# Transposing layer 1's attention probabilities by DMA, as 16-bit word halves, in place of TensorE

## The chip, the cores and the metric

The kernel runs on one core of one Trainium2 chip. The metric is the device time of one execution in microseconds (us), taken as the median of the runs. All arithmetic is in 32-bit floats.

## The reference, cut to what matters

Two layers run one after the other on 128 graphs of 64 nodes with 768 features each. Layer 0 is a graph attention layer with 12 heads, a gate and a layer norm. Layer 1 is a masked attention with 6 heads of size 128, an output projection, a residual and a layer norm. The change lies in layer 1 alone:

```
q = _heads(seq_inputs @ Wq + bq)
k = _heads(seq_inputs @ Wk + bk)
v = _heads(seq_inputs @ Wv + bv)
scores = einsum('bhqd,bhkd->bhqk', q, k) / sqrt(HEAD_SIZE)
bias = where(graph_mask, 0.0, NEG)[:, None]
probs = softmax(scores + bias, axis=-1)
ctx = einsum('bhqk,bhkd->bhqd', probs, v)
ctx = ctx.transpose(0, 2, 1, 3).reshape(B, S, H)
out = layernorm(x + ctx @ Wf + bf)
```

TensorE contracts over the partition dimension. The softmax leaves the probabilities with queries on the partitions, and the context product contracts over keys, so the probabilities have to be transposed between the two.

## The kernel before, in words

The 8192 nodes are 64 tiles of 128 nodes (two graphs each), 32 pairs of tiles, and for layer 1 16 groups of four tiles (`GT = 4`). Layer 0 comes first and spills its result, the result transposed, and layer 1's values to DRAM (`x1_d`, `x1T_d`, `v_d`). Layer 1 then takes one group after another. The large products use block schemes with fewer multiplications than the plain ones: `Job` (seven products for four output blocks) for the output projection, `Wide` (15 products, the table `WIDE`) for q and k.

**The order of the work is written by hand** (`tc.manual_schedule()`, line 171): each engine and each DMA queue executes what it is given in program order, and waits in place for what an instruction needs. The unit of that order is one call of `step(job, i)` (line 306): the product `i` of a job goes to TensorE, then the way out of PSUM of the product before it goes to ScalarE or VectorE, then every running side generator is advanced once. A side that yields once per call is therefore counted in ticks, and a tick is one product.

For a group `g` there are two loops. `woven` (line 695) makes 14 steps, the seven products each of two output jobs of group `g - 1`. The loop at line 1229 makes 30 steps, 15 products each for q and k of group `g + 1`. `attention(g, ticks)` (line 602) runs beside both: its ticks 0 to 13 lie beside the output products, its ticks 14 to 43 beside the q and k products. For the first group there is no `woven` loop: its attention runs from tick 0 beside the 30 q and k steps of group 1, with a table of its own, `TICKS_0`. For the last group the table is `TICKS_N`.

`Attention` (line 490) is one pair of heads; there are three of them to a group (`HK = 3`), called head pair 0, 1 and 2 below. `PARTS` (line 101) lists its parts and `TICKS` (line 102) gives the tick of each part for each head pair:

- `v`: eight DMA loads of the values from SyncE (SP).
- `sp`: the scores, 16 small products on TensorE into a PSUM bank of the tag "m", which has two banks.
- `sc`, `ex`, `mult`: bias, maximum, exponential (ScalarE, line 538), sum and division, the rest on VectorE. The result is the tile `sc`, 128 partitions by 512 words, in SBUF.
- `sT` (line 547): four TensorE transposes of 128x128 words into a PSUM bank.
- `scT` (line 556): one ScalarE copy of that bank to the SBUF tile `scT`, which has two buffers.
- `cp` (line 560): the context products on TensorE, from `v` and `scT`.
- `ctx` (line 577): four ScalarE copies with bias to `ctxT`, the operand of the output projection.

Other sides run beside it. `mask(g)` (line 1192) loads the adjacency from SP and builds the bias eight ticks later. `finish` (line 679) does the layer norm of the output pairs of the loop before; each norm ends with a ScalarE activation (line 327) and a store from SP (line 677) that waits for it. `next_rows` (line 1199) loads the operands of the next group's q and k products. `residuals` (line 614) loads the residual and forms operand sums of the output job. `last_weight` (line 1171) runs once, beside group 0's attention: it loads the four blocks of `wf` into the place of `wv` and makes four sums of them on VectorE (`weight_sums`, line 214), which the first output job needs.

All DMAs of layer 1 are issued by SP, in program order. ScalarE also carries the first write of each q and k block out of PSUM (`Wide.way_out`, line 449), whose banks ("y" and "z", three each) TensorE needs back.

Of the kernel before, what the change touches and what calls it, by code (L numbers as in the profile page):

```python
# [8 lines left out]

F32 = mybir.dt.float32  # L10
U8 = mybir.dt.uint8
AF = mybir.ActivationFunctionType
ALU = mybir.AluOpType
AX = mybir.AxisListType

P = 128
# [15 lines left out]
GT = 4  # L32
# [65 lines left out]
LAST_AT = {7.5: 8, 3: 3, 4: 4, 5: 5, 6: 6, 7: 7, 8: 9, 9: 10, 11: 12, 12: 13, 15: 15, 16: 17, 19: 18}  # L98


PARTS = ("v", "sp", "sc", "ex", "mult", "sT", "scT", "cp", "ctx")
TICKS = [
# [3 lines left out]
]  # L106

TICKS_0 = [
# [3 lines left out]
]  # L112

TICKS_N = [
# [23 lines left out]
def kernel(  # L138
# [21 lines left out]
    nc = tc.nc  # L160
# [7 lines left out]
    dram = ctx.enter_context(tc.tile_pool(name="dram", bufs=1, space=bass.MemoryType.DRAM))  # L168
# [4 lines left out]
    V, S, G, T = nc.vector, nc.scalar, nc.gpsimd, nc.tensor  # L173
# [6 lines left out]
    x1T_d = [dram.tile([P, KC, PAIR * P], F32, name=f"x1Td_{p}") for p in range(NP)]  # L180
    v_d = [dram.tile([P, D], F32, name=f"vd_{t}") for t in range(2 * NP)]
    dst_d = [dram.tile([P, H0], F32, name=f"dstd_{t}") for t in range(2 * NP)]
    wide_d = {k: [dram.tile([P, 2, W2], F32, name=f"wided_{k}{n}") for n in range(NW)] for k in "qk"}


# [152 lines left out]
    pools = {}  # L338
# [151 lines left out]
    class Attention:  # L490
# [43 lines left out]
        def ex(self):  # L534
            V.tensor_tensor(  # L535
                self.sc3, self.sc3, self.mx.unsqueeze(2).to_broadcast([P, 2 * GT, N]), ALU.subtract
            )
            S.activation(self.sc_, self.sc_, AF.Exp, scale=SCALE)  # L538

# [16 lines left out]
        def scT(self):  # L556
            self.scT_ = pools["late"].tile([P, GT * P], F32, tag="scT", name=f"scT_{self.name}")
            S.copy(self.scT_, self.sT_)

        def cp(self):  # L560
            self.cp_ = [bank("m", f"cp_{self.name}_{a}") for a in range(2)]
            for i in range(GT):
                for gr in range(2):
                    at = slice(i * P + gr * N, i * P + (gr + 1) * N)
                    for a in range(2):
                        rows = slice(a * N, (a + 1) * N)
                        for half in range(2):
                            e = slice(half * N, (half + 1) * N)
                            T.matmul(  # L569
                                self.cp_[a][e, at],  # L570
                                self.v_[rows, i, gr, e],
                                self.scT_[rows, at],
                                start=True,
                                stop=True,
                            )
# [23 lines left out]
                        bias=bias_c["v"][:, hd : hd + 1],  # L599
                    )  # L600

    def attention(g, ticks):

        heads = [Attention(g, f) for f in range(HK)]
        for tick in range(max(max(t) for t in ticks) + 1):
            for part in range(len(PARTS)):
                for head, t in zip(heads, ticks):
                    if t[part] == tick:
                        getattr(head, PARTS[part])()
            yield  # L610

    ys, outs = {}, {}
# [1 line left out]
    def residuals(g, last):  # L614

        sb, early = pools["late"], pools["early"]
        if last:
            y4 = early.tile([P, KC, GT * P], F32, tag="qT", name=f"y_{g}", bufs=1)
            y4 = y4.rearrange("p a b -> p (a b)").rearrange("p (i d) -> p i d", d=D)
        for pr in range(PAIR):  # L620
            p = 2 * g + pr
            y = y4[:, 2 * pr : 2 * pr + 2] if last else sb.tile([P, PAIR, D], F32, tag="y", name=f"y_{p}")
            ys[p] = [y[:, i, :] for i in range(PAIR)]
            for i in range(PAIR):
                nc.sync.dma_start(out=ys[p][i], in_=x1_d[p][:, i, :])
        yield
        yield
        places = iter([f"r{k}{t}" for k in range(HK) for t in range(2)] + ["xs", "xs"])

        def last_sum(i):  # L630
            tag = next(places)
            t = early.tile(
                [P, 2, W2], F32, tag=tag, name=f"so_{tag}_{i}", bufs={"xs": 6, "r00": 2}.get(tag, 1)
            )
            return t.rearrange("p k t -> p (k t)")[:, : HK * P].rearrange("p (k t) -> p k t", k=HK)

        for pr in range(PAIR):
            for y in ys[2 * g + pr]:
                G.tensor_tensor(y, y, pools["bf"], ALU.add)  # L639
            c = ctxT[g][:, pr]  # L640
            outs[2 * g + pr], steps = block_sums(
                V,
                [last_sum(4 * pr + i) for i in range(4)]
                if last
                else sum_tiles(sb, f"so{pr}", P, f"o{2 * g + pr}"),
                c[:, :HK, :P],
                c[:, HK:, :P],
                c[:, :HK, P:],
                c[:, HK:, P:],
            )  # L650
            for s in steps:
                yield
                s()
# [56 lines left out]
    with ExitStack() as ph, ExitStack() as ph_r:  # L710
# [351 lines left out]
        for p in range(NP + 1):  # L1062
# [8 lines left out]
            turn, of_new, of_old = TURNS.get(p, (TURN, {}, {})) if new else (LAST, {}, LAST_AT)  # L1071
# [93 lines left out]
    with ExitStack() as ph:  # L1165
        sb = pools["late"] = ph.enter_context(
            tc.tile_pool(name="sb1", bufs=2, reuse_waits="tile")
        )
        nothing = iter(())

        def last_weight():

            weights["f"] = load_weight(wf, "wc", "wf", ())
            pools["bf"] = sb.tile([P, D], F32, name="bf_bc", bufs=1)
            for block in (B11, B21, B22, T3):
                yield
                yield
                load_block(wf, weights["f"], block)
            nc.sync.dma_start(out=pools["bf"], in_=bf.partition_broadcast(P))
            for s in weight_sums(V, weights["f"]):  # L1180
                for _ in range(3):
                    yield
                s()

        def later(n, side):
            for _ in range(n):
                yield
            yield from side

        biases = {}  # L1190

        def mask(g):

            adjs[g] = load_adj(sb, GT * g, GT, f"adjg_{g}")
            for _ in range(8):
                yield
            biases[g] = mask_bias(g)

        def next_rows(g, n):
            if g + 1 < NG:  # L1200
                load_rows_of(g + 1, *NEXT_X.get(n, ()))


        masking = mask(0)
        kT = feature_tile("k", 0)
        rows = Rows("0k", row_blocks[0])
        rows.ready(2)
        keys = Wide("k", 0, rows, kT)
        qk[0] = jobs["q"].dst, kT
        for n in range(NW):  # L1210
            step(keys, n)
            rows.ready(n + 4)
            next_rows(0, n)
            next(masking, None)
        attend, done = attention(0, TICKS_0), nothing
        for g in range(1, NG):
            last = g == NG - 1
            rows = Rows(g, row_blocks.pop(g))
            rows.ready(2)
            pair = {key: Wide(key, g, rows, None) for key in "qk"}  # L1220
            sides = [
                attend,
                done,
                later(14, residuals(g - 1, False)) if g > 1 else last_weight(),
                mask(g),
            ]
            if g == 1:
                sides.append(later(20, residuals(0, False)))
            for n in range(NW):
                for key in "qk":  # L1230
                    step(pair[key], n)
                    for s in sides:
                        next(s, None)
                    if (n, key) == (0, "q"):
                        qk[g] = [feature_tile(key, g) for key in "qk"]
                        pair["q"].dst, pair["k"].dst = qk[g]
                rows.ready(n + 4)
                next_rows(g, n)
            drain(*sides)
            attend = attention(g, TICKS_N if last else TICKS)  # L1240
            if last:
                attend = chain(attend, residuals(g, True))
            p = 2 * g - 2
            woven((out_job(p), out_job(p + 1)), *[attend] * (1 + last))
            if last:
                drain(attend)
            done = finish(p, p + 1)
        p = 2 * NG - 2
        pair = out_job(p), out_job(p + 1)
        woven(pair, done, done, order=ENDS[:9])  # L1250
        drain(done)
        done = finish(p)
        woven(pair, done, done, order=ENDS[9:-1])
        n0, n1 = norm(p + 1, 0), norm(p + 1, 1, last_half=0)
        step(pair[1], ENDS[-1][1])
        next(n0)
        next(n1)
        drain(done)
        flush()
        next(n0, None)  # L1260
        next(n1)
        next(n1, None)
# [42 lines left out]
```

## Time and profile before

| What | Value |
|---|---|
| Time before, median of 3 runs | 2927.09 us (2926.3 to 2927.21) |
| Time of the profiled execution | 2928.25 us |
| Span of the profiled execution | 2926.4 us |
| Granted TensorE clock, mean | 0.997 |
| TensorE (PE) busy | 2881.9 us, 98% |
| VectorE (DVE) busy | 1927.0 us, 66% |
| GpSimd (POOL) busy | 1020.8 us, 35% |
| ScalarE (ACT) busy | 988.4 us, 34% |
| DMA moved | 311.60 MB, mean 106 GB/s |
| TensorE transposes of the probabilities (line 550) | 192, busy 28.9 us |
| ScalarE copies of them (line 558) | 48, 567 to 589 ns each |

The span is the time of the profile from the first to the last instruction; 1.85 us of the profiled execution's own time lie outside it. Layer 1's first attention starts at about 1560 us of the span, so layer 1 takes the last 1366 us. Of an engine that is busy nearly all the time, what a removed instruction gives back is the distance between the starts of its neighbours, not the duration of the instruction, because consecutive products overlap at their ends.

### The profile page before, as it was taken

What the parts mean: (1) busy time and instruction counts of PE and PEld (TensorE: products, weight loads), DVE (VectorE), ACT (ScalarE), POOL (GpSimd) and SP (SyncE); (2) the same over time, 40 slices, a digit from 0 to 9 for tenths busy, and PEclk for the clock granted to TensorE, in tenths of its full rate; (3) what the DMA queues carried; (4) which work ended last, traced back from release to release, by engine and by line L of the source; (5) the groups of instructions that cost most, each with busy time, mean ns of one, the idle gap of its engine ahead of it and who ended that gap; (6) DMA issues with size and microseconds to landing.
All of it is one profiled execution on the core that took longest, in us unless ns stands there. A gap on an engine that the chain in (4) does not pass through costs nothing.

```text
span 2926.4 us, 45671 instructions
## 1 busy us (share of the span) xinstructions
PE 2881.9 (98%) x17856; PEld 1984.6 (68%) x17856; DVE 1927.0 (66%) x3045; ACT 988.4 (34%) x1761; POOL 1020.8 (35%) x857
## 2 busy tenths in 40 slices
PE   7999999999999999999999999999999999999998
PEld 4565565666666665666668777887777887777885
DVE  6888788887888878888764455454465454465445
ACT  2444443444444444444433211222211222212222
POOL 2434354343544434333344132332122332122321
PEclk9999999999999999999999999999999999999999
DMA  5344443444444443334444112222112222122221
GB/s 174 116 145 135 135 142 125 139 140 142 138 132 140 147 132 112 111 115 128 131 152 133 60 55 80 88 84 73 57 59 79 88 82 75 50 63 81 87 66 73
DMA packets 212102, 311.60 MB, mean 106 GB/s; under 512 B 50480, under 2 KB 138544, under 8 KB 211888
## 3 DMA queue, kind: packets, MB, share of 16 engines
q1 hardware_dynamic: 211888, 308.68, 32.8%
q8 instruction: 142, 2.33, 0.3%
q14 instruction: 72, 0.59, 0.1%
HBM read 188.26 MB, written 107.35 MB: 101 GB/s over the span
## 4 chain that ended last, share of the span: by engine, by line
PE 85%; DVE 9%; ACT 2%; DMA 2%; issue 1%; POOL 0%; SPq 0%; POOLq 0%; DVEq 0%; ACTq 0%
PE z_k L440 9%; PE y_o L271 9%; PE z_q L440 8%; PE y_h L271 8%; PE y_g L271 6%; PE y_v L271 6%; PE y_q L440 6%; PE y_k L440 6%; PE z_o L271 4%; PE z_h L271 4%; PE z_v L271 3%; PE z_g L271 2%; PE x_o L271 2%; PE x_g L271 2%; PE cp L569 2%; PE sp L514 2%
## 5 line engine op out<-in xcount | busy, mean ns | idle before, releaser
L538 ACT ACTIVATE sc<-sc 128x512 f32<-128x512 f32 x48 | 30.2, 630 | 757.2 <-DVE sc L535 757.2
L323 POOL TENSOR_TENSOR rs_b<-ve_b,minus_half 128x1 f32<-128x1 f32 x64 | 35.2, 550 | 660.6 <-DVE ve_b L321 598.5
L455 DVE TENSOR_TENSOR qT<-qT,z_q 128x512 f32<-128x512 f32 x96 | 65.8, 685 | 235.2 <-PE z_q L440 235.1
L440 PE MATMUL z_q<-xs,w_wq 128*128 128x256 f32 x896 | 213.5, 381 | 0.3 <-POOL xs L404 0.3
L639 POOL TENSOR_TENSOR y<-y,bf_bc 128x768 f32<-128x768 f32 x64 | 123.6, 1952 | 246.4 <-DMA y<-x1d 246.4
L440 PE MATMUL z_k<-xs,hw_wk 128*128 128x256 f32 x840 | 200.0, 381 | 0.0
L971 POOL TENSOR_TENSOR x<-gate,x 128x768 f32<-128x768 f32 x64 | 117.6, 1837 | 220.8 <-ACT gate L1022 206.5
L404 POOL TENSOR_TENSOR xs<-r,r 128x512 f32<-128x512 f32 x112 | 155.1, 1402 | 100.0 <-PE z_k L440 64.7
L440 PEld LDWEIGHTS z_q<-xs,w_wq 128*128 128x128 f32 x896 | 167.5, 190 | 23.6 <-POOL xs L404 0.7
L844 POOL TENSOR_TENSOR th<-th,wsd 128x768 f32<-128x768 f32 x64 | 117.4, 1834 | 165.8 <-DVE th L843 165.8
L440 PEld LDWEIGHTS z_k<-xs,hw_wk 128*128 128x128 f32 x840 | 158.3, 190 | 21.9
L663 DVE TENSOR_TENSOR y<-y_o,y 128x384 f32<-128x384 f32 x128 | 71.2, 556 | 147.5 <-PE y_o L271 147.5
L323 POOL TENSOR_TENSOR rs_a<-ve_a,minus_half 128x1 f32<-128x1 f32 x64 | 35.9, 562 | 340.9 <-DVE ve_a L321 340.9
L271 PE MATMUL y_h<-w_wq,xT 128*128 128x384 f32 x384 | 136.5, 492 | 8.8 <-DMA w_wq<-in_w_dram 8.2
L271 PE MATMUL y_v<-wv,sv_v 128*128 128x384 f32 x384 | 136.0, 490 | 6.3 <-DVE sv_v L242 4.3
L271 PE MATMUL y_h<-w_wq,sx_x 128*128 128x384 f32 x384 | 136.5, 492 | 4.2 <-ACT h L804 4.2
L271 PE MATMUL y_v<-wv,x1T 128*128 128x384 f32 x384 | 137.7, 496 | 1.8 <-ACT x1T L921 1.0
L271 PE MATMUL y_g<-hw_wk,sx_x 128*128 128x384 f32 x384 | 136.4, 492 | 2.4 <-DVE hw_wk L220 2.2
L271 PE MATMUL z_h<-w_wq,sx_x 128*128 128x384 f32 x384 | 137.8, 495 | 0.0
L271 PE MATMUL z_v<-wv,sv_v 128*128 128x384 f32 x384 | 137.4, 494 | 0.0
L843 DVE TENSOR_TENSOR th<-th,wsd 128x768 f32<-128x768 f32 x64 | 67.7, 1057 | 103.5 <-ACT th L842 103.5
L271 PE MATMUL z_g<-hw_wk,sx_x 128*128 128x384 f32 x384 | 134.4, 486 | 0.0
(179 smaller groups left out, 6672.3 us busy)
## 6 DMA issues: line engine op xcount, KB each, us to landing
x<-in_x_dram SPq DMA_DIRECT2D x64, 384.0 KB, 3.7
dd<-dstd SPq DMA_DIRECT2D x128, 192.0 KB, 3.5
x1d<-x SPq DMA_DIRECT2D x64, 384.0 KB, 2.6
x1Td<-x1T SPq DMA_DIRECT2D x32, 768.0 KB, 4.5
vd<-v SPq DMA_DIRECT2D x64, 384.0 KB, 2.9
r<-x1Td SPq DMA_DIRECT2D x96, 256.0 KB, 3.1
v<-vd SPq DMA_DIRECT2D x384, 64.0 KB, 2.3
y<-x1d SPq DMA_DIRECT2D x64, 384.0 KB, 5.7
```

The lines of the kernel that those rows point to most:

```text
L271: T.matmul(to[:, : self.n], lhsT, rhs, start=kc == 0 and not more, stop=kc == HK - 1, skip_group_check=more,)
L323: G.tensor_tensor(rstd, ve, minus_half, ALU.pow)
L404: G.tensor_tensor(t, self.of(x[0]), self.of(x[2]), x[1])
L440: T.matmul(b[:, half * W2 : (half + 1) * W2], w[:, kc, half * P : (half + 1) * P], x[:, kc, :], start=half == kc == 0 and not more, stop=k ...
L455: V.tensor_tensor(at, at, b.rearrange("p (h t) -> p h t", h=2), ALU.add if sign > 0 else ALU.subtract,)
L514: T.matmul(self.sp_[gr * N : (gr + 1) * N, (i * 2 + a) * N : (i * 2 + a + 1) * N], qT[:, 2 * self.f + a, at], kT[:, 2 * self.f + a, at], s ...
L569: T.matmul(self.cp_[a][e, at], self.v_[rows, i, gr, e], self.scT_[rows, at], start=True, stop=True,)
L639: G.tensor_tensor(y, y, pools["bf"], ALU.add)
L663: V.tensor_tensor(at(*mn), b, at(*mn), ALU.add)
L843: V.tensor_tensor(th[:, 0, :], th[:, 1, :], wsd[:, 0, :], ALU.mult)
L844: G.tensor_tensor(th[:, 1, :], th[:, 1, :], wsd[:, 1, :], ALU.mult)
L971: G.tensor_tensor(xp, st[t]["gate"], xp, ALU.mult)
```

## The change

For groups 0 to 14 the parts `sT` and `scT` are replaced by four others. A 32-bit word is treated as two 16-bit halves, which are only moved and never computed with:

- `split`: two ScalarE copies take the low and the high halves of the probabilities apart. They go from `sc` (read with a step of two halves) to `scT`, which holds 512 low halves and then 512 high halves per partition.
- `send`: one DMA from SP writes the 256 KB to a DRAM buffer, `halves_d`, of which there is one for each head pair.
- `turn`: two transposing DMAs from SP, one for each half, read 512 rows of 128 halves and write 128 partitions of 512 halves over the tile `sc`.
- `join`: two ScalarE copies put the halves together again as words in `scT`.

`cp` then reads `scT` as before. `attention` takes the list of parts as an argument; the last group keeps the old parts and its old table (`PARTS_N`, `TICKS_N`). In `TICKS`, head pair 2 has its context product at tick 24 instead of 22 and its last copies at 25 instead of 23; its split stands at tick 16. `TICKS_0` is spread out: context products at 11, 14 and 20 instead of 6, 10 and 14. `last_weight` starts eight ticks later, and its sums follow each other after two ticks instead of three.

```
-PARTS = ("v", "sp", "sc", "ex", "mult", "sT", "scT", "cp", "ctx")
+PARTS = ("v", "sp", "sc", "ex", "mult", "split", "send", "turn", "join", "cp", "ctx")
 TICKS = [
-    (0, 1, 2, 3, 5, 6, 7, 15, 16),
-    (3, 4, 5, 6, 8, 9, 10, 19, 20),
-    (16, 7, 8, 9, 11, 17, 18, 22, 23),
+    (0, 1, 2, 3, 5, 6, 7, 9, 13, 15, 16),
+    (3, 4, 5, 6, 8, 9, 10, 12, 17, 19, 20),
+    (16, 7, 8, 9, 11, 16, 17, 19, 23, 24, 25),
 ]
 TICKS_0 = [
-    (0, 0, 0, 1, 2, 3, 4, 6, 7),
-    (0, 0, 0, 2, 4, 5, 6, 10, 11),
-    (8, 0, 0, 3, 6, 8, 9, 14, 15),
+    (0, 0, 0, 1, 2, 3, 4, 6, 10, 11, 12),
+    (0, 0, 0, 2, 4, 5, 6, 8, 12, 14, 15),
+    (12, 0, 0, 3, 6, 12, 13, 15, 19, 20, 21),
 ]
+PARTS_N = ("v", "sp", "sc", "ex", "mult", "sT", "scT", "cp", "ctx")
...
+    halves_d = [dram.tile([2, GT, P, P], U16, name=f"halvesd_{i}") for i in range(3)]
...
+        def halves(self, t, joined):
+            u = t.bitcast(U16)
+            return u.rearrange("p (e h) -> p h e" if joined else "p (h e) -> p h e", h=2)
+
+        def split(self):
+            self.scT_ = pools["late"].tile([P, GT * P], F32, tag="scT", name=f"scT_{self.name}")
+            self.flat = self.sc_.rearrange("p i a m -> p (i a m)")
+            for h in range(2):
+                S.copy(self.halves(self.scT_, False)[:, h], self.halves(self.flat, True)[:, h])
+
+        def send(self):
+            nc.sync.dma_start(
+                out=halves_d[self.f].rearrange("h i p c -> p h i c"),
+                in_=self.halves(self.scT_, False).rearrange("p h (i c) -> p h i c", c=P),
+            )
+
+        def turn(self):
+            for h in range(2):
+                nc.sync.dma_start_transpose(
+                    out=self.halves(self.flat, False)[:, h],
+                    in_=halves_d[self.f][h].rearrange("i p c -> (i p) c"),
+                )
+
+        def join(self):
+            for h in range(2):
+                S.copy(self.halves(self.scT_, True)[:, h], self.halves(self.flat, False)[:, h])
...
             for s in weight_sums(V, weights["f"]):
-                for _ in range(3):
-                    yield
+                yield
+                yield
                 s()
...
-                later(14, residuals(g - 1, False)) if g > 1 else last_weight(),
+                later(14, residuals(g - 1, False)) if g > 1 else later(8, last_weight()),
...
-            attend = attention(g, TICKS_N if last else TICKS)
+            attend = attention(g, TICKS_N, PARTS_N) if last else attention(g, TICKS)
```

More of the change, by code (lines that the diff above doesn't have):

```diff
@@ L11 @@
 U8 = mybir.dt.uint8
+U16 = mybir.dt.uint16
 AF = mybir.ActivationFunctionType
@@ L600, in ctx, with attention @@
                     )
-    def attention(g, ticks):
+    def attention(g, ticks, parts=PARTS):
         heads = [Attention(g, f) for f in range(HK)]
         for tick in range(max(max(t) for t in ticks) + 1):
-            for part in range(len(PARTS)):
+            for part in range(len(parts)):
                 for head, t in zip(heads, ticks):
                     if t[part] == tick:
-                        getattr(head, PARTS[part])()
+                        getattr(head, parts[part])()
             yield
```

## The prediction, on record before the changed kernel ran

> **What bounds the kernel now.** I read first the busy tenths of the page, then the busy time by stage over one group, then the timelines of TensorE, ScalarE and SP in that group (its output products start at 2063.3 us of the span).
>
> ```profile
> PE   7999999999999999999999999999999999999998
> ACT  2444443444444444444433211222211222212222
> PEclk9999999999999999999999999999999999999999
> ```
>
> TensorE is full at full clock. The stage view (columns: window, length, then busy time of PE, PEld, DVE, ACT, POOL) splits a group into ticks 0 to 13, ticks 14 to 24 and the rest:
>
> ```profile
> 2063.30:2095.10 31.80, 31.80 (x189) 19.54 (x189) 18.09 (x32) 2.95 (x5) 0.00 (x0) 1.00 0.04 9
> 2095.10:2119.00 23.90, 23.90 (x288) 20.45 (x287) 6.95 (x23) 17.01 (x37) 7.15 (x8) 1.00 0.23 84
> 2119.00:2151.00 32.00, 32.00 (x150) 28.18 (x149) 20.32 (x27) 1.68 (x4) 17.67 (x11) 1.00 0.40 129
> ```
>
> TensorE has no gap in all three, so any TensorE work taken out shortens the group. ScalarE, a third busy on average, is busy 17.0 of 23.9 us in the middle window; that is where the new copies can collide.
>
> TensorE's timeline shows the price of a set of transposes (start, length, group):
>
> ```profile
> 2101.60 1.89 PE L440 MATMUL z_k<-xs,hw_wk 128*128 128x256 f32 x8
> 2103.33 0.60 PE L550 MATMUL sT<-ident,sc 128*128 128x128 f32 x4
> 2103.77 1.89 PE L440 MATMUL z_q<-xs,w_wq 128*128 128x256 f32 x8
> ```
>
> A product costs 1.73 us (2101.60 to 2103.33), the four transposes 0.44 us (2103.33 to 2103.77), not the 0.60 of their row. Beside output products it is 0.44 as well, and a tick there is 1.94 us.
>
> SP's and ScalarE's timelines show the stretch where head pair 2 must be turned:
>
> ```profile
> 2099.93 5.13 SPq L502 DMA_DIRECT2D v<-vd  x8
> 2105.80 0.34 SPq L677 DMA_DIRECT2D out_dram<-y  x1
> ```
>
> ```profile
> 2099.88 1.57 ACT L595 ACTIVATE ctxT<-cp,bv_c 128x256 f32<-128x256 f32 x4 [0.19 <-PE cp L569]
> 2101.80 0.84 ACT L465 ACTIVATE qT<-z_q,bq_c 128x256 f32<-128x256 f32 x2 [0.36 <-PE z_q L440]
> 2103.53 0.84 ACT L465 ACTIVATE kT<-z_k,bk_c 128x256 f32<-128x256 f32 x2 [0.89 <-PE z_k L440]
> 2104.26 0.59 ACT L558 COPY scT<-sT 128x512 f32<-128x512 f32 x1
> 2104.73 1.04 ACT L327 ACTIVATE y<-y,sh_b,rs_b 128x768 f32<-128x768 f32 x1
> ```
>
> SP's eight value loads for pair 2 start only when pair 0's context products end (2099.9, a buffer comes free), and hold SP for 5.1 us.
>
> **What the Trainium skill says.** "TensorE: Matmul & The Clock Gate", Part 4: a TensorE transpose took some 275 ns in a kernel; the trace agrees (273 ns each), yet four in a row cost the stream 0.44 us. "DMA: Bandwidth & Descriptors", section Two DMAs through the same engine are not ordered: a DMA that reads what another wrote must wait for its completion. So `turn` holds SP until `send` has landed. Prices for a transposing DMA: the same page, Latency and other measured facts, 261 GB/s measured in one kernel; "VectorE: DVE Perf Modes", The three transpose paths, 1309 ns for 128x128 of two bytes. The trace of before holds none.
>
> **The change, part by part.**
>
> *TensorE work removed.* 14 groups x 3 sets x 0.44 = 18.5 us. Group 0: 3 x 0.44 = 1.3 us, and its first set waits for VectorE: the product before starts at 1569.72, so ends its slot at 1571.45; the one after starts at 1574.12; 2.67 - 0.44 = 2.2 us of stall go too. Sum 22.0 us, all on the path. The last group is unchanged.
>
> *ScalarE.* One copy of 587 ns goes, four come. Nearest rows: that copy, and the exponential of 512 words from SBUF at 630 ns; I take 0.6, so 1.2 us for a split and for a join (0.8 if the two overlap as the 256-wide pairs do, 1.6 if half-word steps are slow). Net 1.8 us x 45 = 81 us on ScalarE, hidden where ScalarE is idle: pairs 0 and 1 split in ticks 6 and 9, in the window with 2.95 of 31.8 us busy.
>
> *One transposed pair of halves, time T from SP's first `turn` to the landing of both.* By bandwidth: 256 KB at 261 GB/s is 1.0 us, plus two issues at 0.6 us (the value loads' row) plus 2.3 us (their median landing) = 4.5 us, my value. Below: two issues at 0.32 us and a landing of 2.2 us, 2.8 us. Above: 8 tiles x 1.309 us = 10.5 us one after another. Neither end can be a gain by itself.
>
> *Send.* 256 KB; loads of 256 KB (`r`) land in 3.0 us, 2.5 to 5.9. I take 3.1 us from issue.
>
> *Pair 0.* Its split follows the exponential of pair 1 on ScalarE (2079.64 + 0.63), so 2080.3 to 2081.5; send landed 2084.7; turn landed 2089.2. `join` must end before the context products' place, 2098.7 less two sets = 2097.8, so start by 2096.6: T may be 11.9 us. *Pair 1.* Split 2088.5, send landed 2091.7, turn 2096.2; its context products stand at 2107.3 less three sets = 2106.0, so T may be 13 us. While `join` waits, only later splits, layer-norm activations and the first writes from tick 15 on are queued behind it on ScalarE; none is due.
>
> *Pair 2.* In before's clock from pair 0's context products on: split 2099.9 to 2101.1 (it waits for the same products to free `scT`). On SP: value loads to 2105.1, send landed 2108.2, then the two turns. On TensorE, ticks 16 to 24 are nine products at 1.73 us, one set of context products (1.09) and small entry costs from 2099.77: without the set at 2103.33 the place of the last context products is 2116.8, so `join` must start by 2115.6. T may be 7.4 us. ScalarE's own queue: context copies to 2102.7, two first writes and pair 1's join to 2105.6, two norms, two first writes and four context copies to 2110.9, three first writes and a norm to 2114.9: `join` could run from 2114.9 to 2116.1, 0.7 us early. VectorE and the PSUM banks see first writes about 1 us later than now; tick 19 needs a bank written out at 2103.5 for a product at 2105.1, so nothing waits.
>
> *SP, moved past.* Sends and turns stand in front of the adjacency (tick 14, used at tick 22), the stores (nobody waits within the group) and the `r` and residual loads (issued from 2117.9, behind the last store as now, 1 to 2 us later; the residual that they bring is added by POOL, which is idle there). Value loads of pairs 0 and 1 are issued before the sends. DMA engines carry 9 to 129 GB/s here; 45 x 0.52 MB is 24 MB more of 312.
>
> *Group 0.* Pair 0's split ends near 1576.0, send 1579.1, turn 1583.6, join 1584.8; its context products stand at 1571.45 + 8 x 1.73 = 1585.3. Cost 0 at T = 4.5, 3 us at T = 7.4. The last block of `wf` now stands behind pair 2's turn on SP: value loads to 1591.6, send landed 1594.7, turns issued to 1595.9, block landed (4.9 us) at 1601; VectorE reaches the sum near 1598 and waits 3 us (before: 1.6), with its PSUM ways out behind it. I put 3 us on group 0 altogether (0 to 6).
>
> Sum: 22.0 - 3 = 19 us. On the profiled execution 2928.25 - 19.0 = 2909.2; the median of before is 1.2 us lower, so 2908.1.
>
> **Rivals.** *A, all hidden* as above: 2908.1; own range 2903 to 2914. For it: TensorE has no gap, and T may be 7.4 us against 4.5. Against it: T is seen nowhere in this trace.
>
> *B, part of the gain:* the skill's prices hold but ScalarE, not the DMA, is late for pair 2. If split and join are 1.6 us each, ScalarE is 3 x 0.4 = 1.2 us later there, 0.5 us past its margin of 0.7; 14 x 0.5 = 7 us back: 2915. The 17.0 of 23.9 us speak for it.
>
> *C, no change:* T near 8.7 us. Then pair 2 waits 1.3 us a group, just what three sets give; 2921 to 2933.
>
> *D, slower:* the turn is late for pair 2. One mechanism: the transposing DMAs land after `join`'s place, TensorE stands at the context products of tick 24, and nothing behind them can pass. It decides from T = 8.7 us on. At 10.5 us, the wait is 10.5 - 7.4 = 3.1 us, less 1.3 given, 1.8 x 14 = 25 us, less 3.5 from group 0, plus its 6: 2955. Each further us of T costs 14 us. For it: small pieces of 256 bytes, and one price of the skill leads there.
>
> *E, it does not do what it says:* if TensorE's slots held the transposes for free, removing them would give nothing. The starts 2103.33 and 2103.77 exclude that; I give it no chance of its own.
>
> **How the numbers follow.** A 0.52, B 0.09, C 0.13, D 0.26. A measurement of this kernel tells about 0.2%, 5.9 us, from no change; A and B are faster, C the same, D slower. So faster 0.61, same 0.13, slower 0.26. Range 2902 (A without group 0's cost, and 3 us of other waits gone) to 2958 (D at T near 10.7); left out are some 0.05 below and 0.12 above.
>
> **What would show it.** Right: 12 transposes left on line 550, TensorE still without a gap in ticks 14 to 25, TensorE's busy time lower by some 20 us, landing of pair 2's turn under 7 us after its issue, ScalarE near 1070 us. Wrong: a TensorE wait at the context products released by ScalarE's `join`, itself released by a DMA (D or C), or by a busy ScalarE (B); a gap in the first q and k steps of group 0; or SP issues of turns far above 0.6 us each.

## The result and the profile after

The changed kernel takes 2905.32 us (median of 4 runs, 2904.88 to 2907.64), the kernel before 2926.82 us (4 runs). The ratio is 0.9928, with a 95% interval of 0.9911 to 0.9945: 21.5 us or 0.7% faster. 2908.1 us was predicted. The profiled execution took 2904.88 us, of which the span is 2903.1.

The busy tenths of the changed kernel's page, the same three lines as before:

```profile
PE   7999999999999999999999999999999999999998
ACT  2344444444444444444433312333312333312232
PEclk9999999999999999999999999999999999999999
```

TensorE is as full as it was, only for a shorter time. ScalarE shows threes where layer 1 had twos. The group shown before now runs from 2051.9 us to 2138.5 us. In the view by stage (window, length, busy time of PE, PEld, DVE, ACT, POOL, clock, DMA share, GB/s) the windows end with tick 13, with tick 24 and with the group (the middle window of before ran 0.6 us further, into tick 25):

```profile
2051.90:2082.80 30.90, 30.90 (x181) 18.75 (x180) 18.09 (x32) 5.23 (x9) 0.00 (x0) 1.00 0.17 42
2082.80:2105.60 22.80, 22.80 (x281) 19.44 (x279) 7.28 (x23) 18.24 (x39) 7.14 (x8) 1.00 0.35 111
2105.60:2138.50 32.90, 32.90 (x159) 28.99 (x153) 20.12 (x26) 2.88 (x8) 17.67 (x11) 1.00 0.40 127
```

PE is again equal to the length of each window: nothing that was added made TensorE wait. The group itself, from one first output product to the next, took 87.91 us before and takes 86.59 us now; the 14 groups agree in this to 0.01 us, and the difference of 1.32 us is three sets of 0.44. ScalarE has gone from 21.6 to 26.4 us a group, and in the middle window it is now busy for 18.2 of 22.8 us. The timelines show the place of the old transposes of pair 2 (TensorE, with the context products of pair 2), and the path of pair 2's probabilities on SP and ScalarE (start, length, group):

```profile
2089.32 1.89 PE L444 MATMUL z_k<-xs,hw_wk 128*128 128x256 f32 x8
2091.04 1.89 PE L444 MATMUL z_q<-xs,w_wq 128*128 128x256 f32 x8
...
2104.51 1.16 PE L602 MATMUL cp<-scT,v 64*64 64x64 f32 x64
```

```profile
2087.64 5.87 SPq L506 DMA_DIRECT2D v<-vd  x8
2093.61 0.54 SPq L577 DMA_DIRECT2D halvesd<-scT  x1
2094.24 0.52 SPq L710 DMA_DIRECT2D out_dram<-y  x1
2096.45 2.45 SPq L584 DMA_TRANSPOSE sc<-halvesd  x2
```

```profile
2087.69 1.14 ACT L574 COPY scT<-sc 128x512 uint16<-128x512 uint16 x2 [0.35 <-issue]
...
2101.17 0.84 ACT L469 ACTIVATE qT<-z_q,bq_c 128x256 f32<-128x256 f32 x2
2101.90 1.38 ACT L591 COPY scT<-sc 128x512 uint16<-128x512 uint16 x2
2103.14 1.02 ACT L331 ACTIVATE y<-y,sh_b,rs_b 128x768 f32<-128x768 f32 x1
```

The product after `z_k` starts 1.72 us later, where 2.17 us with the transposes lay between. The split follows pair 0's context products, the send follows the value loads, the turn follows the landing of the send, 2.8 us after its issue. The join starts at 2101.90 without a wait for the DMA and is done at 2103.28, 1.2 us before the context products start at 2104.51.

Since the products run without gaps, the span can be cut at TensorE's own marks. Layer 0 goes up to the first scores, group 0 to the first output product after them, and the last stage to the end:

| Profiled execution | First scores at | Group 0 | Groups 1 to 15, us |
|---|---|---|---|
| Before | 1563.14 | 60.62 | 1302.64 |
| After | 1559.84 | 59.11 | 1284.15 |
| e1_tables_only | 1559.19 | 62.31 | 1302.70 |
| e2_no_turn | 1560.20 | 57.11 | 1284.19 |
| e3_turn_late | 1558.16 | 62.17 | 1313.37 |
| e4_copies_twice | 1563.61 | 65.54 | 1302.05 |
| e5_weight_first | 1561.74 | 58.29 | 1284.17 |
| e6_four_turns | 1560.08 | 67.45 | 1284.77 |
| e7_products_early | 1563.12 | 59.52 | 1289.46 |

The first column differs by up to 5.5 us between executions, though layer 0 is the same in all of them; so 3.3 us of the difference between the two profiles is no effect of the change. The last column repeats to 0.1 us where a kernel has no new wait there. It gives 18.5 us, group 0 gives 1.5 us.

### The profile page after: what moved, and what is told of

Its sections match the earlier page's. It is cut to its first block, busy times and chain, and to the rows that moved or that the text cites. A ratio compares the mean times of both kernels' runs of the same rounds, so it can differ in the third digit from the quotient of the medians.

```text
span 2903.1 us, 45587 instructions
## 1 busy us (share of the span) xinstructions
PE 2860.5 (99%) x17676; PEld 1965.3 (68%) x17676; DVE 1930.0 (66%) x3045; ACT 1060.0 (37%) x1896; POOL 1022.1 (35%) x857
## 4 chain that ended last, share of the span: by engine, by line
PE 84%; DVE 9%; ACT 2%; DMA 2%; issue 2%; POOL 1%; SPq 1%; POOLq 0%; DVEq 0%; ACTq 0%
PE y_o L275 9%; PE z_k L444 8%; PE z_q L444 8%; PE y_h L275 7%; PE y_g L275 6%; PE y_v L275 6%; PE y_k L444 5%; PE y_q L444 5%; PE z_o L275 4%; PE z_h L275 4%; PE z_v L275 3%; PE z_g L275 3%; PE x_o L275 2%; PE x_g L275 2%; PE sp L518 2%
```

## The experiments

The theory: TensorE sets the time, each set of transposes taken off it gives 0.44 us, and the way round by DMA costs nothing as long as the join of pair 2 ends before tick 24's context products. The rivals: the gain comes from the looser tables; part of the gain is lost again on ScalarE, SP or the DMA engines; and, against the condition on the join, the landing of the turn or the load of ScalarE has no bearing.

**e1, the tables alone.** The changed kernel with the old parts in the new tables (the row of pair 2 is shown, the others likewise):

```
-PARTS = ("v", "sp", "sc", "ex", "mult", "split", "send", "turn", "join", "cp", "ctx")
+PARTS = ("v", "sp", "sc", "ex", "mult", "sT", "scT", "cp", "ctx")
...
-    (16, 7, 8, 9, 11, 16, 17, 19, 23, 24, 25),
+    (16, 7, 8, 9, 11, 17, 18, 24, 25),
```

> The new tick tables and the later sums of wf stay (context products of pair 2 at tick 24, group 0 spread out), but the TensorE transposes and the ScalarE copy take the place of split, send, turn and join again. Theory (the gain is TensorE time, 0.44 us a set): the 45 sets come back, 19.8 us, and group 0's first set waits for VectorE again, 2.2 us: 2925 to 2928 us, as before. Rival (the gain comes from the looser tables, which free PSUM banks and ScalarE): stays at 2905 to 2912.

Measured: 2927.14 us, ratio to before 0.9999 (0.9990 to 1.0007). Groups 1 to 15 take 1302.70 us, the kernel before 1302.64. The tables give nothing; the 18.5 us are the transposes. Group 0 waits 2.0 us for VectorE at its first transpose again. That this group is 1.7 us longer than in the kernel before is the clock, not the tables: behind this wait two products are 2.66 and 2.49 us from start to start instead of 1.73, and the granted clock of these 5.2 us is 0.67. The kernel before has the same wait of 2.0 us, and its clock stays at 1.00 behind it. The three lines are e1's:

```profile
1569.71 0.63 PE L554 MATMUL sT<-ident,sc 128*128 128x128 f32 x4 [2.04 <-DVE sc L549]
1570.17 2.86 PE L444 MATMUL z_q<-xs,w_wq 128*128 128x256 f32 x8
1572.83 2.65 PE L444 MATMUL z_k<-xs,hw_wk 128*128 128x256 f32 x8
```

**e2, no transposing at all.** The context products take the probabilities as they stand:

```
-PARTS = ("v", "sp", "sc", "ex", "mult", "split", "send", "turn", "join", "cp", "ctx")
+PARTS = ("v", "sp", "sc", "ex", "mult", "none", "none", "none", "copy", "cp", "ctx")
...
+        def none(self):
+            pass
...
+        def copy(self):
+            self.scT_ = pools["late"].tile([P, GT * P], F32, tag="scT", name=f"scT_{self.name}")
+            S.copy(self.scT_, self.sc_.rearrange("p i a m -> p (i a m)"))
```

> Leaves the transposing out altogether: the context products take the probabilities as they stand, through one ScalarE copy from sc to scT at the join's tick; no split, no send, no turn. So the context is that of untransposed probabilities. Theory (all that was added is hidden but for a wait of group 0): 2903 to 2905.5 us, TensorE in groups 1 to 14 the same to a microsecond. Rival (part of the 22 us is lost again to ScalarE, SP or DMA traffic): faster than the changed kernel by 5 us or more.

Measured: 2905.9 us, ratio 0.9929 (0.9915 to 0.9944), the same as the changed kernel. Groups 1 to 15 take 1284.19 us against 1284.15. So the three ScalarE copies more, the send and the two turns that the changed kernel has for each pair of heads cost nothing in these groups. Group 0 is 2.0 us shorter than in the changed kernel.

**e3, the turn of pair 2 late.**

```
-    (16, 7, 8, 9, 11, 16, 17, 19, 23, 24, 25),
+    (16, 7, 8, 9, 11, 16, 17, 23, 23, 24, 25),
```

> The turn of pair 2 is issued at tick 23 instead of 19, behind the store of tick 22, which waits for a norm on ScalarE that ends at about 5 us after the turn's issue now. Nothing else moves. Theory (the turn lands 3.75 us after its issue, and the join must start some 6.65 us after the issue it has now): turn issued 5.1 us later, join ends 2.2 us after the place of the context products, TensorE waits 2.2 us in each of 14 groups: 31 us, 2936 us (2930 to 2943). Rival (the landing of the turn isn't what the context products depend on in time): 2905 to 2908.

Measured: 2939.06 us, ratio 1.0045 (1.0028 to 1.0062), slower than before the change. Groups 1 to 15 take 29.2 us more than in the changed kernel: 1.9 to 2.0 us in 12 of the 14 groups, where 2.2 were expected, and 2.3 and 3.5 us in the other two. In the group with 3.5 us, one product behind the wait took 3.43 us instead of 1.83 at a granted clock of 0.52. In one of the 12 groups, the timeline of ScalarE, then of TensorE:

```profile
2112.08 0.84 ACT L469 ACTIVATE qT<-z_q,bq_c 128x256 f32<-128x256 f32 x2
2115.28 0.76 ACT L591 COPY scT<-sc 128x512 uint16<-128x512 uint16 x1 [2.36 <-DMA sc<-halvesd]
2116.43 0.76 ACT L591 COPY scT<-sc 128x512 uint16<-128x512 uint16 x1 [0.39 <-DMA sc<-halvesd]
```

```profile
2117.24 1.26 PE L602 MATMUL cp<-scT,v 64*64 64x64 f32 x64 [1.74 <-ACT scT L591]
```

SP issued this turn at 2112.56, so the halves were to be had 2.7 and 3.9 us later. The chain is the one foretold for the slower case: the join waits for a DMA, the context products wait for the join, and nothing passes them. Another 3.1 us was lost in group 0, whose table this edit leaves alone. There TensorE waits 2.2 us for VectorE where it waits 1.8 us in the changed kernel, and behind that wait two products take 1.7 us more at a granted clock of 0.67. The rest are shorter waits for VectorE, whose second sum of `wf` took 3.00 us instead of 1.35; why it did is open.

**e4, every half-word copy made twice.**

```
-            for h in range(2):
+            for h in (0, 1, 0, 1):
                 S.copy(self.halves(self.scT_, False)[:, h], self.halves(self.flat, True)[:, h])
```

and the same in `join`.

> Each of the four half-word copies on ScalarE is made twice with the same result. Theory (ScalarE is the next thing late for pair 2: its join ends 1.2 us before the context products' place): split of pair 2 and joins of pairs 1 and 2 add 3.5 us to ScalarE's queue there, 0.9 of it taken up by its one idle stretch, so TensorE waits 1.4 us in each of 14 groups: 20 us, 2925 us (2915 to 2932). Rival (ScalarE, a third busy, has room for it): 2905 to 2908.

Measured: 2928.86 us, ratio 1.0005 (0.9997 to 1.0014): the whole gain is gone. Groups 1 to 15 take 17.9 us more, 1.3 us in each of 14, and group 0 takes 6.4 us more, 1.7 us of it at a granted clock of 0.67 behind a wait of 2.2 us and the rest in waits for ScalarE and VectorE. ScalarE's and TensorE's timelines of one group:

```profile
2117.85 1.16 ACT L331 ACTIVATE y<-y,sh_b,rs_b 128x768 f32<-128x768 f32 x1
2118.77 0.97 ACT L469 ACTIVATE qT<-z_q,bq_c 128x256 f32<-128x256 f32 x2
2119.48 2.76 ACT L591 COPY scT<-sc 128x512 uint16<-128x512 uint16 x4
```

```profile
2122.30 1.26 PE L602 MATMUL cp<-scT,v 64*64 64x64 f32 x64 [0.97 <-ACT scT L591]
```

Here the turn (issued 2113.27) had long landed. ScalarE has no idle time in front of the join and is late by its own work. It is 39% busy in this run.

**e5, wf ahead of the turn.** In the changed kernel TensorE waits once in group 0, 1.8 us, behind VectorE, which waits 5.2 us (idle time before the first sum) for the last block of `wf`. VectorE, then TensorE in the changed kernel:

```profile
1600.97 1.36 DVE L221 TENSOR_TENSOR wf<-wf 128x1152 f32<-128x1152 f32 x1 [5.18 <-DMA wf<-in_wf_dram]
```

```profile
1615.39 1.99 PE L444 MATMUL z_q<-r,w_wq 128*128 128x256 f32 x8 [1.77 <-DVE qT L459]
```

The edit loads the block earlier:

```
+            yield
+            yield
             for s in weight_sums(V, weights["f"]):
...
-                later(14, residuals(g - 1, False)) if g > 1 else later(8, last_weight()),
+                later(14, residuals(g - 1, False)) if g > 1 else later(6, last_weight()),
```

> In group 0 the four blocks of wf are loaded two ticks earlier (8, 10, 12, 14), so that the last stands on SP ahead of pair 2's turn and not behind it; the sums stay at ticks 18, 20, 22 and 24. Theory (the one wait of TensorE left in group 0, 1.8 us on VectorE's q sums, comes from VectorE waiting for that block): the block lands some 4 us earlier, VectorE waits under 2 us at the first sum, and group 0 (from its first scores to the first output product) takes 57.1 to 57.4 us instead of 59.1, as in the run without turns; 2903.5 us in all, too little for the clock to tell. Rival (VectorE is overfull there anyway): 59 us again.

Measured: 2906.91 us, ratio 0.9932 (0.9919 to 0.9944), no different from the changed kernel. Half of what was expected came: VectorE's idle time before the sum fell to 2.5 us, its hold on TensorE is gone, and group 0 takes 58.3 us. But SP's queue was held longer by the loads, pair 2's turn was issued 36.4 us after the first scores instead of 34.3, and TensorE now waits 1.05 us for the join. One wait took the place of the other.

**e6, four turns of half the size.**

```
             for h in range(2):
-                nc.sync.dma_start_transpose(
-                    out=self.halves(self.flat, False)[:, h],
-                    in_=halves_d[self.f][h].rearrange("i p c -> (i p) c"),
-                )
+                for j in range(2):
+                    nc.sync.dma_start_transpose(
+                        out=self.halves(self.flat, False)[:, h, j * W2 : (j + 1) * W2],
+                        in_=halves_d[self.f][h, 2 * j : 2 * j + 2].rearrange("i p c -> (i p) c"),
+                    )
```

> Each turn is issued as four transposing DMAs of 256 rows instead of two of 512. Tells what the 1.24 us that SP is held by one of them depends on. If on its rows: 0.62 us each, the turn lands as before. If it is a fixed price: 1.24 us each, SP held 5.0 us per turn and the last lands 6.2 us after the first issue, which leaves pair 2 just 0.4 us; 2905 to 2912 us in both cases.

Measured: 2914.58 us in a single run. The issues of the line of the turn in the changed kernel, then in this one (count, then shortest, median and longest in ns):

```profile
L584 SPq DMA_TRANSPOSE sc<-halvesd x90: 1122/1242/2142, 1575.5 to 2789.7; - x90
```

```profile
L585 SPq DMA_TRANSPOSE sc<-halvesd x180: 1109/1233/2328, 1575.7 to 2801.8; - x180
```

Half the rows hold SP just as long: between these two sizes the price is per DMA. Groups 1 to 15 take 1284.77 us, so even with the last quarter issued 3.7 us after the first, pair 2 is in time (two groups are 0.2 us longer). Nearly all the rest of the loss is in group 0, 8.3 us, which was not foreseen. There the eight small turns of pairs 0 and 1 hold SP for 11.2 us, where four took 5.2, so the turn of pair 2 is issued 40.2 us after the first scores instead of 34.3. TensorE waits 5.1 us for the join, and the granted clock of the next 4.8 us is 0.58.

**e7, pair 2's products back at tick 22.**

```
-    (16, 7, 8, 9, 11, 16, 17, 19, 23, 24, 25),
+    (16, 7, 8, 9, 11, 16, 17, 19, 21, 22, 23),
```

> Pair 2's join, context products and last copies go back two ticks, to 21, 22 and 23, where the products stood before the change. Tells how much slack pair 2 has. Theory (second half lands 3.75 us after the turn's issue; ScalarE has nothing to do ahead of the join then): join ends within 0.3 us of the products' place, 0 to 4 us in 14 groups, 2905 to 2910 us. Rival (the prediction's own sum, T of 4.5 us and a turn issued 3.1 us after the send): the join ends 1.5 us late, 21 us, 2926 us.

Measured: 2914.41 us, ratio 0.9958 (0.9945 to 0.9971). Groups 1 to 15 take 5.3 us more than in the changed kernel, a little over the 0 to 4 expected and far from the rival's 21; the other 3.7 us by which the profiled executions differ lie in layer 0 (3.3) and group 0 (0.4). The profile names a wait of TensorE for the join in 5 groups, up to 1.5 us and 3.4 us in all; group by group, 11 of the 14 are longer than in the changed kernel, by 0.05 to 1.65 us. So pair 2 is at its limit there, and the two ticks are worth about 5 us.

## Why the prediction was right, step by step

*TensorE work removed.* 18.5 us for 14 groups was forecast from the 0.44 us between two starts; 18.5 us were measured (1302.64 - 1284.15), and e1 and e2 show from both sides that it is the transposes and all of them. The row's duration of 0.60 us a set would have given 25 us.

*Group 0.* The forecast was a gain of 3.5 us less a cost of 3 us; it gained 1.5. e2, which has neither transposes nor turns, separates the two: the gain is 3.5 us (60.62 - 57.11), the cost 2.0 us (59.11 - 57.11). The cost came about as foretold, through the last block of `wf` and VectorE, but its size is partly luck. Counted from the first scores, the block was forecast to land after 37.9 us, and VectorE's first sum, which waited for it, started after 41.1 us. Two terms were off: the send of pair 2 landed 4.9 us after its issue, where 3.1 were taken, and its two turns held SP for 2.4 us, where 1.2 were taken. VectorE waited 5.2 us instead of 3, but only 1.8 us of that reached TensorE, where the forecast passed all of it on. (The 3 us that pair 0 would cost at T = 7.4 were a slip: the forecast's own terms give 2.4. T came out lower, so the case did not arise.)

*T, the open price.* Taken at 4.5 us (2.8 to 10.5). In e3, the cleanest place, it is 3.9. The terms were off in opposite directions. The first issue was put at 0.6 us, the price of a value load, and is 1.24. From the start of the second issue to its landing 3.9 us were put (0.6 + 1.0 + 2.3), and the median of the 90 turns is 2.5:

```profile
DMA to landing us min/median/max: 2.3/2.5/4.2
```

So T is 1.24 + 2.5 = 3.7 us. The landing of 2.3 us that the forecast took from the value loads already counts from the start of an issue, so its sum holds one issue too many (in e3 the second half was to be had 2.6 us after the start of its issue); that the two errors partly cancel is luck. The upper bound, eight tiles at the Trainium skill's 1309 ns ("VectorE: DVE Perf Modes", The three transpose paths) one after another, is excluded: eight tiles turn in under 4 us here, issue and landing included. The send landed in 2.6 us (median), 3.1 were taken.

*Pair 2 decides.* The limit for T was put at 7.4 us. In the group shown, a join of 1.4 us must start by 2103.1, 6.65 us after the turn's issue at 2096.45; T leaves some 2.8 us of that. The slack is in fact a little larger, because the first copy of the join can run while the second half is still landing and only the second copy, 0.77 us, has to wait for it: 2104.5 - 0.8 - (2096.45 + 3.9) makes some 3.4 us. e3 bears this out, where the turn is issued 5.2 us later and the products start 1.8 us later, and so does e7, which takes 3.45 us away (two products) and just begins to lose. e3 thereby tested the slower rival: its mechanism holds, its threshold was not reached.

*ScalarE.* A split takes 1.12 to 1.14 us and a join 1.38 to 1.41, where 1.2 was taken for each. The join was forecast to end 0.7 us before the products; it ends 1.2 us before. In all, ScalarE has 71.6 us more (988.4 to 1060.0), 81 were forecast. The sum of the lengths would be larger still, 45 x (1.13 + 1.39 - 0.59) = 87 us; busy time grows by less because copies overlap their neighbours on ScalarE, as the join at 2101.90 does the activation before it, which ends at 2102.01. Rival B's mechanism is real as well: in the group of e4 that is shown, the split is 1.0 us longer and the two joins 1.2 and 1.4 us, and the products start 1.3 us late.

*SP moved past.* Nobody waits for the adjacency, the stores or the loads behind the turns in groups 1 to 14: e2, which has no turns, is no shorter there.

*The signs that were named.* Twelve transposes are left (line 554), TensorE is busy for 21.4 us less (2881.9 to 2860.5), and no gap stands in ticks 14 to 25 or in group 0's first q and k steps. One sign of being wrong did appear: SP is held by a turn for twice the 0.6 us that were taken. It did no harm, because the landing behind it is shorter than was taken.

*The total.* 19 us were forecast, 20.0 us belong to layer 1 in the profiles (18.5 and 1.5); the missing 1 us is group 0's cost, 2 us instead of 3. The difference of the medians, 21.5 us, includes what layer 0 varies by.

## What to carry to other kernels

Where an engine has no gap, price a removed instruction by the distance between the starts of its neighbours, and cut the span at that engine's own marks: here this told 0.1 us where whole runs differ by several. Work moved from a full engine to a long way round is free only up to a due time, so find the one consumer with the least slack, and add up every in-order queue on the way to it; an average of 37% busy said nothing on ScalarE, which had 1.2 us to spare where it counted, while the landing of the turn had 3.4. Turn as much as possible with one transposing DMA: of the two sizes tried, the smaller held SP just as long.

## What was new of the hardware

- A transposing DMA of two-byte words holds SP for 1.24 us, with 512 rows or with 256; the plain ones beside it are issued in 0.32 to 0.6 us (medians line by line).
- 128 KB turned through DRAM to SBUF land 2.5 us after the issue (2.3 to 4.2), about as a plain load of 64 KB does (2.3 us).
- A ScalarE copy of 512 half-words takes 612 ns when it reads with a step of two, and 767 ns when it writes with a step of two (medians); e2's copy of 512 whole words without a step takes 611 ns.
- A store of 256 KB in pieces of 256 bytes lands in 2.6 us (median; 4.9 at most), as one of 384 KB in rows of 3 KB does.
- Behind five waits of TensorE, of 1.7, 2.0, 2.2, 2.2 and 5.1 us (e3, e1, e3, e4, e6), the granted clock fell to 0.52 to 0.67 for 3.5 to 5.2 us, which cost 1.6 to 1.9 us each time. Behind others as long, of 2.04 us in the kernel before and 2.11 us in e3, it stayed at 1.00. What decides between the two is not shown.
